# Two-layer attention kernel: the last projection's input turned by VectorE and memory instead of TensorE

## The chip, the cores and the metric

The kernel runs on one core of a Trainium2 chip, in float32. The metric is the device time of one execution in microseconds. The core has five engines with their own instruction streams: TensorE (PE, matmuls; PEld is its weight load), VectorE (DVE), ScalarE (ACT), GpSimd (POOL) and SyncE (SP), which here only issues DMAs.

## The reference

Two layers over the same 8192 tokens of 512 channels. The change concerns the end of the second layer:

```
x = layer0(x)                     # group norm, 8-head attention over 1024 tokens, residual
# layer 1, for each of 8 images (b) of 1024 positions:
x_ln = layernorm(x); q = x_ln @ wq + bq
o = gelu(depthwise 7x7 conv of q, stride 2); offsets = 1x1 conv of o; sample x at 256 points
k, v from the samples; att = softmax(q_h k_h^T) v_h       # 8 heads of 64
z = att @ mo_w + mo_b + x
out = gelu(layernorm(z) @ mlp_w + mlp_b) + z
```

## The kernel before, in words

There are two passes. The first computes layer 0 for all images and leaves its output in memory (mid) and a normalised copy (hat_d). The second pass, where the change is, works on 16 half images (hi) of 512 positions and in each on 4 pairs of heads, so on 64 units. Unit n takes a pair of heads: scores (TensorE), the row maxima (VectorE), exponentials (ScalarE), then `moved`: the 128x1024 exponentials are transposed by VectorE in 32x32 blocks into sq, written to memory (sq_d) and read back (et) so that keys lie on partitions. This happens twice a unit, for the two heads. `share` and `spread` do the same with the sums of the softmax (rsT, rs_d, inv). `product` (av) multiplies et by the values, and `scale` writes attH. The tiles et and sq have two buffers each.

What follows attention for a half image is done four units later, one tile of 128 positions per unit, by `back_steps`: `fetch` and `add` bring the residual (xr), `joined` multiplies attH by wo, adds xr into z and takes mean and variance on VectorE, the power on GpSimd; `norm` makes zn; `turned` transposes zn with four TensorE transposes and two ScalarE copies into zT; `mlp` multiplies zT by wm; `biased`, `gelu` and `end` finish. The last half image is done after the last unit ("tail").

Nothing is scheduled by priority. Each step is put into a list with a place (`at(place, step)`), the list is sorted by place, and each engine and each DMA queue runs its instructions in that order. In unit n the scores stand at n, the transposes and moves of the two heads at n+0.02 and n+0.04, the sums between them, wo at n+0.05, the next queries (wqq) at n+0.06, zn at n+0.13, av of unit n at n+1.1, `turned` at n+0.6, and `mlp` at n+1.03, right behind the scores of unit n+1. Convolution fills, keys and values for the next image stand between av and the scores of some units. In every queue an instruction that waits holds up all behind it; SyncE issues sq_d, et, rs_d, inv, xr and the loads of the next operands.

All instructions pass one helper, line 54, so the profile names them by tile.

Of the kernel before, what the change touches and what calls it, by code (L numbers as in the profile page):

```python
# [9 lines left out]
F32 = mybir.dt.float32  # L10
I32 = mybir.dt.int32
AF = mybir.ActivationFunctionType
ALU = mybir.AluOpType
# [4 lines left out]
P = 128  # L18
# [3 lines left out]
C = 512  # L22
NC = C // P
# [11 lines left out]
SQ = 32  # L35
NSQ = P // SQ
# [30 lines left out]
class Attention:  # L67
# [14 lines left out]
    @staticmethod  # L82
    def by_blocks(keys):

        return keys.rearrange("p (j q s) -> p s j q", s=NSQ, q=SQ)
# [104 lines left out]
class MovedAttention(Attention):  # L190
# [34 lines left out]
    def part(self, et, v, half, first):  # L225
        if half == 0 and first:
            self.av = self.ps_av.tile([P, QB], F32, tag="av", name="av")
        av = self.av[:, ts(half, 2 * P)].rearrange("p (n r q) -> p r n q", n=2, q=SQ)
        for j in range(0 if first else NQT, NQT if first else NT):
            for h in range(2):  # L230
                self.nc.tensor.matmul(
                    av[ds(h * HD, HD)],
                    lhsT=v[not first][:, j % NQT, ds(h * HD, HD)],
                    rhs=et[:, h, :, j],
                    start=(j == 0),
                    stop=(j == NT - 1),
                )
# [3 lines left out]
def attention_then_deformable_attention(  # L241
# [30 lines left out]
    nc = tc.nc  # L272
# [4 lines left out]
    dram = ctx.enter_context(tc.tile_pool(name="dram", bufs=1, space=DRAM))  # L277
# [4 lines left out]
    ident = const.tile([P, P], F32, tag="ident", name="ident")  # L282
# [7 lines left out]
    def mm_tile():  # L290
        return ps_mm.tile([P, QB], F32, tag="mm", name="mm")

    def by_chunk(w):
        return w.rearrange("(c p) o -> p c o", p=P)

    def load_w(pool, w, name):
        t = pool.tile([P, NC, w.shape[1]], F32, tag=name, name=name)
        nc.sync.dma_start(t, by_chunk(w))
        return t
# [43 lines left out]
    def rstd(dst, var, eps):  # L343
        nc.vector.tensor_scalar(dst, var, eps, None, ALU.add)
        nc.gpsimd.tensor_tensor(dst, dst, minus_half[:, 0 : dst.shape[1]], ALU.pow)

    def project(lhsT, rhs):
        ps = mm_tile()
        out = ps[:, 0 : rhs(0).shape[-1]]
        for c in range(NC):  # L350
            nc.tensor.matmul(out, lhsT=lhsT(c), rhs=rhs(c), start=(c == 0), stop=(c == NC - 1))
        return out
# [4 lines left out]
    def at(place, step):  # L357
        due.append((place, len(due), step))
# [37 lines left out]
    with ExitStack() as l0:  # L396
# [3 lines left out]
        nc = InOrder(tc)  # L400
# [25 lines left out]
        def load_weight(w):  # L426
# [17 lines left out]
            out=g3, in_=g3, pattern=[[-GRP, ng], [0, GRP]], compare_op=ALU.is_ge,  # L444
# [3 lines left out]
            out=g3, in_=g3, pattern=[[GRP, ng], [0, GRP]], compare_op=ALU.is_ge,  # L448
# [318 lines left out]
        for b in range(B):  # L767
            first = b * per
            for hp in range(1, NHP):
                places = first_places if b == 0 else pair_places  # L770
# [17 lines left out]
            for hp in range(NHP):  # L788
                for qt in range(NT):
                    n = first + hp * NT + qt  # L790
                    if n % per == 0 and b > 0:
# [6 lines left out]
                    t = qkv[b, hp]  # L798
# [5 lines left out]
                        q=t["q", qt // NQT][:, ts(qt % NQT, P)],  # L804
                        k=t["k"],
# [7 lines left out]
    with ExitStack() as l1:  # L813
        nc = tc.nc


        def pool(name, bufs=1):
            return l1.enter_context(tc.tile_pool(name=name, bufs=bufs, reuse_waits="tile"))

        first, raw, late, late2, cv, cvhat, wp = (  # L820
            pool(n) for n in ("first", "raw", "late", "late2", "cv", "cvhat", "w2")
        )
        work = pool("work1", 2)
        nc = InOrder(tc)
# [4 lines left out]
        bqq, bvk, bvv, bv_c, bq_c, lng, lnb = (  # L829
            wp.tile([P, NC], F32, tag=n, name=n)  # L830
            for n in ("bqq", "bvk", "bvv", "bv_c", "bq_c", "lng", "lnb")
        )
        dwb = cv.tile([P, NC], F32, tag="dwb", name="dwb")
        dww = cv.tile([P, NC, KS * KS], F32, tag="dww", name="dww")
        pww = cv.tile([P, NC, 2], F32, tag="pww", name="pww")

        def load_small():
            with nc.allow_non_contiguous_dma(reason="small vectors onto partitions"):
                for t, v in (
                    (bvk, mk_b), (bv_c, bv), (bvv, mv_b), (bqq, mq_b), (bq_c, bq), (lng, ln_g),  # L840
                    (lnb, ln_b),
                ):
                    nc.sync.dma_start(t, v.rearrange("(c p) -> p c", p=P))

        def load_conv():
            with nc.allow_non_contiguous_dma(reason="small vectors onto partitions"):
# [221 lines left out]
        def tmp(name, bufs):  # L1068
            return work.tile([P, C], F32, tag=name, name=name, bufs=bufs)

        def back_steps(hi, start, step, tail=False):

            b, half = divmod(hi, 2)
            xs = mid[b].rearrange("(t p e) c -> e t p c", e=2, p=P)[half]
            outs = out_tok[b].rearrange("(t p e) c -> e t p c", e=2, p=P)[half]
            xr, z, zn, zT, res = {}, {}, {}, {}, {}
            n_units = 2 * B * NHP

            def fetch(t):
                xr[t] = tmp("xr", 4)  # L1080
                nc.sync.dma_start(xr[t], xs[t])

            def add(t):
                nc.gpsimd.tensor_tensor(xr[t], xr[t], bo_row, ALU.add)

            def joined(t):
                ps = project(lambda c: attH[hi][:, c, ts(t, P)], lambda c: wo[:, c, :])
                z[t] = tmp("z", 4)
                nc.vector.tensor_tensor(z[t], ps, xr[t], ALU.add)
                stats = work.tile([P, 6], F32, tag="stats", name="stats")  # L1090
                mv = xr["mv", t] = work.tile([P, 3], F32, tag="mv", name="mv")
                nc.vector.bn_stats(stats, z[t])
                nc.vector.bn_aggr(mv[:, 0:2], stats)
                rstd(mv[:, 2:3], mv[:, 1:2], 1e-5)

            def norm(t):
                zn[t], mv = tmp("zn", 2), xr["mv", t]
                nc.vector.tensor_scalar(
                    zn[t], z[t], mv[:, 0:1], mv[:, 2:3], ALU.subtract, ALU.mult
                )  # L1100

            def turned(t):
                ps = mm_tile()
                for c in range(NC):
                    nc.tensor.transpose(ps[:, ts(c, P)], zn[t][:, ts(c, P)], ident)
                zT[t] = tmp("zT", 2)
                for half in range(2):
                    nc.scalar.copy(zT[t][:, ts(half, C // 2)], ps[:, ts(half, C // 2)])

            def mlp(t):  # L1110
                res["ps", t] = project(lambda c: zT[t][:, ts(c, P)], lambda c: wm[:, c, :])

            def biased(t):
                res[t] = tmp("res", 3)
                nc.vector.tensor_tensor(res[t], res["ps", t], bm_row, ALU.add)

            def gelu(t):
                nc.scalar.activation(res[t], res[t], AF.Gelu)

            def end(t):  # L1120
                (nc.vector if tail else nc.gpsimd).tensor_tensor(res[t], res[t], z[t], ALU.add)
                (nc.sync if tail else nc.gpsimd).dma_start(outs[t], res[t])

            for t in range(NC):
                over, eve = (start + step * t >= n_units - i and not tail for i in range(2))
                n, pair = start + step * t, start + step * (t - t % 2)

                ends = (n + 0.6, n + 1.03, n + 1.035)
                if eve:
                    ends = (n + 0.61, n + 0.72, n + 0.73) if over else (n + 1.06, n + 1.62, n + 1.625)  # L1130
                places = (pair - 1.6, pair - 0.5), (n + 0.05, n + 0.13), ends
                if tail:
                    turn = n + 0.15 + 0.005 * (t > 0)
                    places = (n - 0.7, n - 0.6), (n, n + 0.01), (turn, n + 0.25, n + 0.26)
                steps = (fetch, add), (joined, norm), (turned, mlp, biased)
                for place, what in zip(sum(places, ()), sum(steps, ())):
                    at(place, lambda t=t, what=what: what(t))


                ends = [t - 1, t] if t % 2 and not tail else [t] if tail else []  # L1140

                for what, after in (
                    (gelu, 0.27 if tail else 0.735 if over else 1.72),
                    (end, 0.28 if tail else 0.74 if over else 2.24),
                ):
                    for i in ends:
                        at(n + after, lambda i=i, what=what: what(i))
# [71 lines left out]
        def load_late():  # L1219
            nonlocal bq_row, wo, wm, bo_row, bm_row  # L1220
            bq_row = load_row(wp, bq, "bq_row")
            wo = load_w(late2, mo_w, "wo")
            wm = load_w(late2, mlp_w, "wm")
            bo_row = load_row(late, mo_b, "bo_row")
            bm_row = load_row(late2, mlp_b, "bm_row")
            load_conv()
# [66 lines left out]
```

## Time and profile before

| | |
|---|---|
| median of 3 runs | 3526.83 us (3524.01 to 3528.84) |
| profiled execution | 3522.86 us, span 3521.2 us, mean granted TensorE clock 0.984 |
| busy, share of the span | PE 96%, DVE 72%, ACT 51%, POOL 44% |
| second pass | about 2200 us to the end; its 64 units from about 2297 us to 3477 us |
| DMA | 641.65 MB in all, mean 182 GB/s |

Times in views are microseconds from the start of the span. A row of the groups gives the operation by tiles (out<-in), the shape, the count, busy time and mean ns of one, and the idle time of the engine before them with what ended it. A row of waits gives the total, the count and the longest. A row of a timeline gives start, length, engine and operation; several equal ones are merged, and in square brackets stands the idle time before it. A float32 matmul shows as two records.

### The profile page before, as it was taken

How to read it: one execution, taken by the hardware profiler on the slowest of the kernel's cores; microseconds unless marked ns; L12 is line 12 of the kernel's file. 1: busy time of each engine (PE TensorE's matmuls, PEld its weight loads, DVE VectorE, ACT ScalarE, POOL GpSimd, SP SyncE). 2: the span in 40 equal slices, each digit the busy share in tenths (PEclk: the TensorE clock that was granted, in tenths of full speed). 3: DMA queues.
4: the chain of work that ended last, by engine and by line, in shares of the span. 5: the costliest groups of instructions: out<-in, count | busy, mean ns of one | idle time of the engine just before them, and what ended most of it. 6: DMA issues, size and time to landing. Idle time of an engine off the chain costs nothing.

```text
span 3521.2 us, 45344 instructions
## 1 busy us (share of the span) xinstructions
PE 3388.6 (96%) x14568; PEld 1679.5 (48%) x14568; DVE 2534.7 (72%) x3373; ACT 1809.8 (51%) x3919; POOL 1536.3 (44%) x1903
## 2 busy tenths in 40 slices
PE   7999999999999999999999998889998989899998
PEld 4544554554554554455455444534444444444443
DVE  4767778888888888788888875257777676665654
ACT  3443355566566566566567562245555455554442
POOL 1001226646636646655654653215445353532222
PEclk9999999999999999999999999899999999999999
DMA  4666667766766666767766667445656555565653
GB/s 145 171 159 176 193 170 195 211 160 184 219 164 186 207 169 185 204 174 194 203 174 175 202 177 208 136 157 194 198 175 196 171 181 178 179 199 189 222 184 123
DMA packets 446589, 641.65 MB, mean 182 GB/s; under 512 B 77104, under 2 KB 240944, under 8 KB 444304
## 3 DMA queue, kind: packets, MB, share of 16 engines
q1 hardware_dynamic: 415712, 536.67, 52.4%
q0 software_dynamic: 29488, 100.00, 9.5%
q8 instruction: 116, 1.90, 0.2%
q10 hardware_dynamic: 1152, 2.10, 0.2%
q14 instruction: 121, 0.99, 0.1%
HBM read 246.38 MB, written 123.73 MB: 105 GB/s over the span
## 4 chain that ended last, share of the span: by engine, by line
PE 81%; POOL 4%; ACT 4%; DVE 4%; issue 3%; DMA 2%; SPq 2%; POOLq 0%; ACTq 0%; DVEq 0%
PE mm L54 51%; PE sc L54 16%; PE av L54 15%; ACT e L54 2%; SPq L54 2%; POOL chunk L54 1%; POOL row L54 1%; DVE chunk L54 1%; ACT L54 1%; DVE nmax L54 1%; POOL oa L54 0%; DMA et<-sq_d 0%; DMA sq_d<-sq 0%; POOL rows L54 0%; POOL hat L54 0%
## 5 line engine op out<-in xcount | busy, mean ns | idle before, releaser
L54 ACT ACTIVATE e<-sc,nmax 128x1024 f32<-128x1024 f32 (+1 forms) x1024 | 802.9, 797 | 597.1 <-DVE nmax L54 595.8
L54 DVE TENSOR_REDUCE nmax<-sc 128x1 f32<-128x1024 f32 (+1 forms) x640 | 751.4, 1215 | 383.7 <-PE sc L54 382.7
L54 DVE STREAM_TRANSPOSE sq<-e 128x1024 f32<-128x1024 f32 x640 | 764.3, 1224 | 241.4 <-ACT e L54 218.2
L54 POOL TENSOR_TENSOR oa<-part_x,oa 128x256 f32<-128x256 f32 x852 | 632.2, 742 | 574.7 <-ACT part_x L54 530.3
L54 PE MATMUL sc<-k,q 64*128 64x512 f32 x2048 | 536.6, 619 | 17.1 <-ACT e L54 15.4
L54 ACT ACTIVATE part_x<-pad_x,dww_x 128x256 f32<-128x256 f32 x852 | 434.9, 541 | 222.9 <-POOL oa L54 221.3
L54 PE MATMUL av<-et,v 128*64 128x256 f32 x4096 | 503.5, 388 | 13.9 <-DMA et<-sq 13.0
L54 PE MATMUL mm<-xT,wqkv 128*128 128x512 f32 x1024 | 470.6, 604 | 3.1 <-issue 3.1
L54 PEld LDWEIGHTS av<-et,v 128*64 128x64 f32 x4096 | 275.3, 137 | 319.2 <-issue 161.2
L54 POOL TENSOR_TENSOR chunk<-parts,chunk 128x256 f32<-128x256 f32 x240 | 179.9, 749 | 384.3 <-ACT parts L54 369.2
L54 PEld LDWEIGHTS sc<-k,q 64*128 64x128 f32 x2048 | 186.5, 187 | 280.0 <-issue 190.7
L54 PEld LDWEIGHTS mm<-xT,wqkv 128*128 128x128 f32 x1024 | 187.1, 190 | 240.3 <-issue 234.9
L54 POOL TENSOR_TENSOR mv<-mv,minus_half 128x1 f32<-128x1 f32 x128 | 77.3, 604 | 489.2 <-DVE mv L54 487.1
L54 PEld LDWEIGHTS mm<-wqkv,xT 128*128 128x128 f32 x2048 | 234.1, 192 | 25.7 <-issue 25.7
L54 PE MATMUL mm<-wqkv,xT 128*128 128x128 f32 x2048 | 244.8, 278 | 0.0
L54 PE MATMUL mm<-wm,zT 128*128 128x512 f32 x512 | 238.1, 608 | 1.3 <-ACT zT L54 1.0
L54 PE MATMUL mm<-w,attT 128*128 128x512 f32 x512 | 235.5, 604 | 1.7 <-DVE attT L54 1.7
L54 PE MATMUL mm<-wo,attH 128*128 128x512 f32 x512 | 230.8, 593 | 0.4
L54 PE MATMUL mm<-hat_h,wqq 128*128 128x512 f32 x512 | 230.7, 593 | 0.0
L54 DVE SCALAR_TENSOR_TENSOR od<-pad_x,dww_x,od 128x256 f32<-128x256 f32 x276 | 226.4, 820 | 5.5
L54 ACT ACTIVATION_READ_ACCUMULATOR e<-sc,nmax 128x1 f32 x1024 | 209.2, 204 | 0.0
L54 PE MATMUL mm<-w,hat_x 128*128 128x512 f32 x384 | 172.7, 600 | 0.0
(163 smaller groups left out, 3555.4 us busy)
## 6 DMA issues: line engine op xcount, KB each, us to landing
et<-sq SPq DMA_DIRECT2D x2048, 128.0 KB
sq_d<-sq SPq DMA_DIRECT2D x128, 512.0 KB
et<-sq_d SPq DMA_DIRECT2D x128, 512.0 KB
inv<-rs_d SPq DMA_DIRECT2D x256, 128.0 KB
hat_h<-hat_d SPq DMA_DIRECT2D x16, 1024.0 KB
xr<-mid SPq DMA_DIRECT2D x64, 256.0 KB
x<-in_x_dram POOLq DMA_DIRECT2D x60, 256.0 KB
out_dram<-res POOLq DMA_DIRECT2D x60, 256.0 KB
```

The source lines that it names most:

```text
L54: return self.tc.keep_in_program_order(op(*args, **kwargs))
```

## The change

For all but the last half image, `turned` transposes zn on VectorE in 32x32 blocks into zT and writes it to memory (z_d); `back` reads it back into zT so that channels lie on partitions, channel s*128 + c*32 + k on partition 4k + s. wm, lng and lnb are loaded in that order of channels, by four DMAs each. zT holds its four chunks interleaved, so the lhsT of `mlp` is read with a stride of four elements. The last half image keeps the TensorE transposes, with zn and the copies written in the new order. `turned` moves from n+0.6 to n+0.1301 and `back` stands at n+0.3; `mlp` stays, but for the last units.

```diff
+        def by_parts(v):
+            return [
+                v[ts(s, NC * SQ)].rearrange("(c k) o -> k c o" if len(v.shape) > 1 else "(c k) -> k c", k=SQ)
+                for s in range(NSQ)
+            ]
...
-                    (bvk, mk_b), (bv_c, bv), (bvv, mv_b), (bqq, mq_b), (bq_c, bq), (lng, ln_g),
-                    (lnb, ln_b),
+                    (bvk, mk_b), (bv_c, bv), (bvv, mv_b), (bqq, mq_b), (bq_c, bq),
                 ):
                     nc.sync.dma_start(t, v.rearrange("(c p) -> p c", p=P))
+                for t, v in ((lng, ln_g), (lnb, ln_b)):
+                    for s, part in enumerate(by_parts(v)):
+                        nc.sync.dma_start(t[ds(s, SQ, NSQ)], part)
...
             def norm(t):
                 zn[t], mv = tmp("zn", 2), xr["mv", t]
+                out, row = zn[t], z[t]
+                if tail:
+                    out, row = by_blocks(out, "(c k s)"), by_blocks(row, "(s c k)")
                 nc.vector.tensor_scalar(
-                    zn[t], z[t], mv[:, 0:1], mv[:, 2:3], ALU.subtract, ALU.mult
+                    out, row, mv[:, 0:1], mv[:, 2:3], ALU.subtract, ALU.mult
                 )
+            def by_blocks(row, order):
+                return row.rearrange(f"p {order} -> p s c k", s=NSQ, c=NC)
             def turned(t):
-                ps = mm_tile()
-                for c in range(NC):
-                    nc.tensor.transpose(ps[:, ts(c, P)], zn[t][:, ts(c, P)], ident)
                 zT[t] = tmp("zT", 2)
-                for half in range(2):
-                    nc.scalar.copy(zT[t][:, ts(half, C // 2)], ps[:, ts(half, C // 2)])
+                if tail:
+                    ps = mm_tile()
+                    for c in range(NC):
+                        nc.tensor.transpose(ps[:, ts(c, P)], zn[t][:, ts(c, P)], ident)
+                    for half in range(2):
+                        nc.scalar.copy(
+                            part(t)[:, ds(2 * half, 2)],
+                            ps[:, ts(half, C // 2)].rearrange("p (c q) -> p c q", q=P),
+                        )
+                    return
+                nc.vector.transpose(
+                    zT[t].rearrange("p (s q c) -> p s c q", s=NSQ, c=NC),
+                    zn[t].rearrange("p (s c k) -> p s c k", s=NSQ, c=NC),
+                )
+                there = zT["there", t] = dram.tile([P, NSQ, P], F32, tag="z_d", name="z_d", bufs=3)
+                nc.sync.dma_start(there, zT[t].rearrange("p (s x) -> p s x", s=NSQ))
+            def back(t):
+                if not tail:
+                    nc.sync.dma_start(
+                        zT[t].rearrange("p (r x) -> p r x", r=NSQ),
+                        zT["there", t].rearrange("(r k) s x -> (k s) r x", r=NSQ),
+                    )
+            def part(t):
+                return zT[t].rearrange("p (q c) -> p c q", c=NC)
             def mlp(t):
-                res["ps", t] = project(lambda c: zT[t][:, ts(c, P)], lambda c: wm[:, c, :])
+                res["ps", t] = project(lambda c: part(t)[:, c], lambda c: wm[:, c, :])
...
-                ends = (n + 0.6, n + 1.03, n + 1.035)
-                if eve:
-                    ends = (n + 0.61, n + 0.72, n + 0.73) if over else (n + 1.06, n + 1.62, n + 1.625)
+                ends = (n + 0.1301, n + 0.3, n + 1.03, n + 1.035)
+                if eve and not over:
+                    ends = (n + 0.1301, n + 0.3, n + 1.62, n + 1.625)
+                elif over:
+                    ends = (n + 0.1301, n + 0.3, n + 0.72, n + 0.73)
...
-                    places = (n - 0.7, n - 0.6), (n, n + 0.01), (turn, n + 0.25, n + 0.26)
-                steps = (fetch, add), (joined, norm), (turned, mlp, biased)
+                    places = (n - 0.7, n - 0.6), (n, n + 0.01), (turn, turn, n + 0.25, n + 0.26)
+                steps = (fetch, add), (joined, norm), (turned, back, mlp, biased)
...
-            wm = load_w(late2, mlp_w, "wm")
+            wm = late2.tile([P, NC, C], F32, tag="wm", name="wm")
+            for s, part in enumerate(by_parts(mlp_w)):
+                nc.sync.dma_start(wm[ds(s, SQ, NSQ)], part)
```

## The prediction

> **What bounds the kernel now.** I read the page's engine totals and chain first, then for the second pass (windows from 2400 to 3400 us) the groups by shape and the waits of the SyncE queue, and last two units instruction by instruction.
>
> ```profile
> PE 3388.6 (96%) x14568; PEld 1679.5 (48%) x14568; DVE 2534.7 (72%) x3373; ACT 1809.8 (51%) x3919; POOL 1536.3 (44%) x1903
> ```
>
> ```profile
> L54 PE MATMUL mm<-ident,zn 128*128 128x128 f32 x212 | 36.0, 296 | 38.2 <-DVE zn L54 38.2
> ```
>
> TensorE is the bound, and the transposes cost it their own work and 38.2 us of waiting for zn in 53 tiles. SyncE's queue is the second thing to read:
>
> ```profile
> SPq L54 <- DMA sq_d<-sq: 420.4, 106, 9.7
> SPq L54 <- DVE sq L54: 261.0, 46, 11.2
> SPq L54 <- PE av L54: 81.3, 33, 5.3
> ```
>
> SyncE waits 106 times, 4 us each, for a write to memory to land before it may issue the read back, and 33 times for the av products: et has two buffers, so the first et read of unit n needs the end of av of unit n-1. One unit in the queue (3374.50 to the next unit's sq_d):
>
> ```profile
> 3374.50 0.38 SPq L54 DMA_DIRECT2D et<-sq_d  x1
> 3374.93 0.50 SPq L54 DMA_DIRECT2D rs_d<-rsT  x1
> 3375.47 0.42 SPq L54 DMA_DIRECT2D sq_d<-sq  x1
> 3379.99 0.37 SPq L54 DMA_DIRECT2D et<-sq_d  x1
> 3380.40 1.24 SPq L54 DMA_DIRECT2D inv<-rs_d  x2
> 3381.74 1.02 SPq L54 DMA_DIRECT2D xr<-mid  x2
> ```
>
> and the same stretch on TensorE:
>
> ```profile
> 3373.45 1.03 PE L54 MATMUL av<-et,vals 128*64 128x512 f32 x4
> 3374.40 2.08 PE L54 MATMUL mm<-smp,wvk 128*128 128x256 f32 x8
> 3376.32 0.60 PE L54 MATMUL mm<-ident,zn 128*128 128x128 f32 x4
> 3376.85 2.00 PE L54 MATMUL sc<-keys,q 64*128 64x256 f32 x16
> 3378.78 3.70 PE L54 MATMUL mm<-wm,zT 128*128 128x512 f32 x8
> 3382.32 3.60 PE L54 MATMUL mm<-wo,attH 128*128 128x512 f32 x8
> 3385.75 3.60 PE L54 MATMUL mm<-hat_h,wqq 128*128 128x512 f32 x8
> 3389.28 1.94 PE L54 MATMUL av<-et,vals 128*64 128x512 f32 x8
> ```
>
> The et read leaves 0.02 us after av ends (3374.48). The mlp product follows the scores directly, 4.30 us after av's end here. From mlp's start to av's end is 12.44 us of TensorE without a gap.
>
> **What the change removes.** 60 of 64 tiles lose four transposes. From transpose to scores is 0.53 us (3376.32 to 3376.85): 60 x 0.53 = 32 us, and the 38 us of waits. ACT loses 120 copies of 377 ns, off the path.
>
> **What it adds on VectorE.** 60 block transposes of 128x512. sq<-e does 128x1024 in 1224 ns, so 0.61 us; the output here has a stride of four elements, which no row shows, so up to twice that. It follows zn directly, before attH and the convolution taps. VectorE is busy 715 of 1065 us from 2385 to 3450 us, so it has the room, and SyncE comes to the tile later than this (below): nothing taken.
>
> **What it adds on SyncE: a loop.** The issue order puts z_d<-zT and zT<-z_d of unit n behind sq_d, et, rs_d, sq_d, et, inv, inv of unit n. The first et waits for av of unit n-1. TensorE's own order is scores n+1, mlp n, wo, wqq, av n, and mlp n needs zT. So each mlp waits for a chain that starts at the end of the previous av, and each av waits for that mlp. What lies between av and scores (transposes before; keys, values, fills still) can hide in the wait, but the loop itself cannot be shorter than its terms:
>
> - TensorE from mlp to the end of av: 12.44 us.
> - av's end to et: 0.02; et to the end of the second inv issue: 3381.64 - 3374.50 = 7.14, of which 4.52 is the second sq_d landing.
> - z_d, next in the queue: 0.10 later. Write of 256 KB to its landing: the completion events of mid<-xr, 256 KB in the first pass, give 2.85 us; sq_d, 512 KB, gives 4.5. It queues behind an et and two inv still in flight, so 3.7.
> - Queue to the read, 0.10. zT read, 256 KB in 512-byte runs: the inv pairs move as much in such runs in 3.4 to 3.7 us each in the first pass; xr, 256 KB, takes 5.4 behind other reads. The queue ahead is empty then, so 4.0. To TensorE 0.05.
> - The clock. TensorE now idles some 10 us in each loop. What that costs stands in two places of before:
>
> ```profile
> 2558.78 1.12 PE L54 MATMUL mm<-ident,zn 128*128 128x128 f32 x4 [4.33 <-DVE zn L54]
> 2559.82 3.79 PE L54 MATMUL sc<-keys,q 64*128 64x256 f32 x16
> 2563.54 3.80 PE L54 MATMUL mm<-wm,zT 128*128 128x512 f32 x8
> ```
>
> After an idle of 4.33 us the transposes took 1.12 instead of 0.60 and the scores 3.79 instead of 2.00; the granted clock from 2559 to 2562 us is 0.50. That is 2.3 us lost; shorter cases in the trace lost 1.2. I take 2.3 in each loop.
>
> Sum: 12.44 + 0.02 + 7.14 + 0.10 + 3.7 + 0.10 + 4.0 + 0.05 + 2.3 = 29.85 us. Before, 57 loops lie from the mlp of unit 5 (2389.75) to that of unit 62 (3453.18): 1063.4 / 57 = 18.66. So 57 x 11.19 = 638 us more.
>
> The Trainium skill, "DMA: Bandwidth & Descriptors", section "Anatomy of one DMA — SWDGE (gpsimd) path", gives a DMA 2.0 us plus its bytes at 436 GB/s, so, as an estimate, 2.6 us for each of the two. The completion events here say 2.85 and 3.4 at the least; by the page the loop would be 2.5 us shorter and the kernel 143 us faster than my sum.
> The same skill, "TensorE: Matmul & The Clock Gate", section "What's actually happening", reopens the clock after one busy window of about 3.4 us, which would lose 1.7 us in a loop instead of the 2.3 that the rows show: 34 us less.
>
> **Edges.** The first mlp (unit 5) waits until 2391.98 (end of its inv) + 7.9 instead of 2389.75: +10. At the end the last two tiles come 15 and 19 us after the last loop's av, about where the et waits put them before: +2. In the tail four zn write, and eight copies write, with strides: 0 to 1 us a tile, +2. Before the loop, 9 more DMA issues at about 0.5 us stand ahead of later weights: 0 to 4.5, +1. zT is read as lhsT with a stride of four: the weight load of 190 ns hides under a matmul pitch of 430; smp as weights at stride 2 takes 196, so nothing, and up to 1.5 us a unit if it doubled. Together +15.
>
> 3522.86 (profiled execution) + 638 + 15 = 4176; the median of the runs lies 4 us above the profiled one: 4180.
>
> **Rivals.** (1) Faster: the round trip is hidden and TensorE only gets shorter: 3527 - 32 - 38 = 3457. It decides if zT lands within 2 us of av's end (plus what lies between av and scores, 0 to 7 us). For it: 96% TensorE. Against: z_d is not even issued until 7.2 us after av's end. 4%. (2) The latency is exposed but not the queue, as if z_d left at once: wo's end is 6.97 us after mlp's start, zn ends up to 5 us later, then transpose 0.7 and 7.9 for both DMAs: a loop of 20.5, 57 x 1.8 + 15 = +118, 3645. Against it the issue order on SyncE. 6%. (3) The clock stays low for the whole section of TensorE: 12.44 us becomes 24.9, the loop 40, 4750. Against: in the case shown the wo product after 8 us is back at 3.60. 3%. No change (within 0.2%) needs gain and wait to cancel: 1%. My case: 86%.
>
> **Range.** With 2.85, 3.4 and 1.2 us for write, read and clock the loop is 27.3: 4037. With 4.5, 5.4 and a full low stretch of 6.8 us (3.4 lost) it is 33.2: 4375; all three high at once is unlikely, so 4320. Runs agree within 0.2%, which is what can be told from no change.
>
> **What would show it.** Right: the mlp matmuls wait for DMA zT<-z_d in nearly every unit, 8 to 13 us; the et read still 0.02 us after av; z_d 7.2 us after that; unit period 27 to 33 us and nearly constant; granted clock down to some 0.7 in this stage; zn waits gone. Wrong: z_d issued before et, mlp waiting under 3 us, or TensorE still above 90% there.

## The result, and the profile after

The changed kernel takes 4185.43 us (median of 4 runs, 4183.69 to 4190.22) against 3526.45 us: ratio 1.187, 95% interval 1.185 to 1.189. Its profiled execution has a span of 4182.5 us, 661 us more than before, and a mean granted TensorE clock (the share of its full clock that the profile says TensorE was given) of 0.912 instead of 0.984.

The page of after: engine totals, the clock by 40 slices (in tenths), and the chain that ended last, which is followed back from the last instruction, at each step to what released it:

```profile
PE 3468.5 (83%) x14328; PEld 1706.5 (41%) x14328; DVE 2596.6 (62%) x3433; ACT 1775.9 (42%) x3799; POOL 1534.2 (37%) x1903
PEclk9999999999999999999999887887878887787888
PE 72%; DMA 17%; DVE 4%; SPq 3%; issue 2%; POOL 2%; ACT 1%; POOLq 0%; DVEq 0%; ACTq 0%
```

The same line of before:

```profile
PE 81%; POOL 4%; ACT 4%; DVE 4%; issue 3%; DMA 2%; SPq 2%; POOLq 0%; ACTq 0%; DVEq 0%
```

The first pass is as before; from the 23rd slice on the clock is between 0.7 and 0.9 (0.81 on the mean from 2400 to 4060 us), and DMAs, 2% of the chain before, are 17% of it. The waits of TensorE, then of SyncE's queue, from 2400 to 4060 us (total us, times, longest):

```profile
PE mm L54 <- DMA zT<-z_d: 591.1, 56, 16.7
```

```profile
SPq L54 <- PE av L54: 589.5, 55, 14.4
SPq L54 <- DMA sq_d<-sq: 513.4, 111, 10.5
SPq L54 <- DMA z_d<-zT: 220.8, 56, 6.6
```

Two waits of the same length face each other: TensorE waits 591 us for SyncE's read, and SyncE waits 590 us for TensorE's av. That is a loop. One turn of it, on TensorE (the dots stand for lines left out) and on SyncE:

```profile
3302.00 5.29 PE L54 MATMUL mm<-wm,zT 128*128 128x512 f32 x8 [12.79 <-DMA zT<-z_d]
3307.12 3.60 PE L54 MATMUL mm<-wo,attH 128*128 128x512 f32 x8
3310.55 3.60 PE L54 MATMUL mm<-hat_h,wqq 128*128 128x512 f32 x8
3314.08 1.94 PE L54 MATMUL av<-et,vals 128*64 128x512 f32 x8
...
3331.90 5.69 PE L54 MATMUL mm<-wm,zT 128*128 128x512 f32 x8 [11.40 <-DMA zT<-z_d]
```

```profile
3316.04 0.37 SPq L54 DMA_DIRECT2D et<-sq_d  x1
3316.51 0.45 SPq L54 DMA_DIRECT2D rs_d<-rsT  x1
3317.05 0.38 SPq L54 DMA_DIRECT2D sq_d<-sq  x1
3322.30 0.37 SPq L54 DMA_DIRECT2D et<-sq_d  x1
3322.76 1.24 SPq L54 DMA_DIRECT2D inv<-rs_d  x2
3324.09 0.55 SPq L54 DMA_DIRECT2D z_d<-zT  x1
3328.21 0.38 SPq L54 DMA_DIRECT2D zT<-z_d  x1
```

av ends at 3316.02; et leaves 0.02 us later; z_d leaves only at 3324.09, its landing (the completion event of the DMA) releases zT at 3328.21, and mlp starts at 3331.90, 29.90 us after the mlp before it. From the mlp of unit 5 (2404.12) to that of unit 62 (4112.50) lie 57 turns of 29.97 us on the mean.

### The profile page after: what moved, and what is told of

It is laid out like the page before. It is cut to its first block, busy times and chain, and to the rows that moved or that the text cites. A ratio compares the mean times of both kernels' runs of the same rounds, so it can differ in the third digit from the quotient of the medians.

```text
span 4182.5 us, 45127 instructions
## 1 busy us (share of the span) xinstructions
PE 3468.5 (83%) x14328; PEld 1706.5 (41%) x14328; DVE 2596.6 (62%) x3433; ACT 1775.9 (42%) x3799; POOL 1534.2 (37%) x1903
## 4 chain that ended last, share of the span: by engine, by line
PE 72%; DMA 17%; DVE 4%; SPq 3%; issue 2%; POOL 2%; ACT 1%; POOLq 0%; DVEq 0%; ACTq 0%
PE mm L54 47%; PE av L54 13%; PE sc L54 12%; DMA z_d<-zT 6%; DMA sq_d<-sq 5%; DMA zT<-z_d 4%; SPq L54 3%; DVE smp L54 1%; ACT e L54 1%; DVE chunk L54 1%; DVE nmax L54 1%; DVE attH L54 1%; DMA et<-sq 1%; POOL oa L54 0%; POOL rows L54 0%
## 5 line engine op out<-in xcount | busy, mean ns | idle before, releaser
L54 PE MATMUL mm<-wm,zT 128*128 128x512 f32 x512 | 369.3, 886 | 618.3 <-DMA zT<-z_d 616.8
L54 PEld LDWEIGHTS mm<-wm,zT 128*128 128x128 f32 x512 | 160.3, 324 | 805.0 <-issue 765.4
L54 DVE TENSOR_TENSOR res<-mm,bm_row 128x512 f32<-128x512 f32 x64 | 44.2, 691 | 560.1 <-PE mm L54 560.0
L54 ACT ACTIVATE q<-mm,bqq 128x512 f32<-128x512 f32 x64 | 44.0, 688 | 813.8 <-PE mm L54 813.8
```

What stands on the lines that cost most here:

```text
L54: return self.tc.keep_in_program_order(op(*args, **kwargs))
```

## The experiments

The theory (the expectations call it the queue theory): the unit is 30 us long because zT's trip stands in SyncE's queue behind an et read that waits for the previous av. The rivals: the latency of two DMAs in a row wherever they stand; the added traffic; the layout (strided weights and transposes). "Before" is the kernel before in runs on the same chip.

### The trip ahead of the heads' DMAs (e2_order)

`moved` keeps the VectorE transpose; a new step `sent` holds its sq_d write and et read.

```diff
             at(n + 0.02, lambda: att.moved(u, 0))
             at(n + 0.039, lambda: att.share(u["sums"]))
             at(n + 0.04, lambda: att.moved(u, 1))
-            at(n + 0.041, lambda: u.update(inv=att.spread()))
+            at(n + 0.31, lambda: att.sent(u, 0))
+            at(n + 0.32, lambda: att.sent(u, 1))
+            at(n + 0.33, lambda: u.update(inv=att.spread()))
```

> Only SyncE's order is changed: in each unit the writes and reads of the two heads (sq_d, et) and the inv reads are issued behind z_d and zT instead of ahead of them. Queue theory: what makes the unit 30 us is that zT's trip stands behind an et read that waits for the previous av. With it in front, z_d leaves when zT is transposed: mlp to the end of wo 7.0 us, z to the end of the transpose about 4.8, write 4.2, read 3.1, a little for the clock: 19 to 20.5 us a unit, total 3560 to 3660 us. Rival, the latency itself (two DMAs in a row cost what they cost wherever they stand): unchanged, about 4185. Rival, traffic (31 MB more in short runs): unchanged, about 4185.

Measured: 3657.46 us, ratio 1.038 (1.036 to 1.040), inside the range at its upper end. From the scores of unit 5 to those of unit 63 a unit takes 20.38 us. TensorE's waits from 2400 to 3400 us, and SyncE's queue in one unit:

```profile
PE mm L54 <- DMA zT<-z_d: 80.7, 29, 6.8
```

```profile
2932.95 0.32 SPq L54 DMA_DIRECT2D z_d<-zT  x1
2938.29 0.37 SPq L54 DMA_DIRECT2D zT<-z_d  x1
2938.70 0.51 SPq L54 DMA_DIRECT2D sq_d<-sq  x1
2942.28 0.37 SPq L54 DMA_DIRECT2D et<-sq_d  x1
```

The same DMAs with the same bytes cost 528 us less when zT does not stand behind et. Both rivals said that this order would change nothing, and fall as causes of the 660 us. Part of the gain is that the write itself lands sooner here: from z_d's issue to zT's are 2.90 us on the mean instead of 4.50 in the changed kernel. The 134 us over before that are left are what the trip costs in this place, its two DMAs in a row, the clock that the waits let fall and the heads' DMAs that now stand behind it, less what the change saves; this run does not split them.

### The mlp one unit later (e3_later)

```diff
-                ends = (n + 0.1301, n + 0.3, n + 1.03, n + 1.035)
+                ends = (n + 0.1301, n + 0.3, n + 2.03, n + 2.035)
...
-                zT[t] = tmp("zT", 2)
+                zT[t] = tmp("zT", 3)
...
-                zn[t], mv = tmp("zn", 2), xr["mv", t]
+                zn[t] = work.tile([P, C], F32, tag="q", name="zn") if tail else tmp("zn", 1)
+                mv = xr["mv", t]
...
-                    (gelu, 0.27 if tail else 0.735 if over else 1.72),
-                    (end, 0.28 if tail else 0.74 if over else 2.24),
+                    (gelu, 0.27 if tail else 0.735 if over else 2.4),
+                    (end, 0.28 if tail else 0.74 if over else 2.6),
```

> The mlp step of a tile, and what follows it, stands one unit later (behind the scores of unit n+2), with one zT buffer more and one zn buffer less. The DMAs and their order are those of the change. Queue theory: zT lands 15.2 us after av's end and TensorE gets to the mlp 16.3 us or more after it, so the wait on zT goes from 591 us to under 60. SyncE's queue in itself needs about 17 us a unit (four waits for a landing in a row), so the unit is 17.3 to 18.7 us: 3440 to 3540 us in all. Rival, traffic: the same bytes move, so at least half of the loss stays: above 3800 us.

Measured: 3560.03 us, ratio 1.010 (1.007 to 1.013), 20 us over the expected range; a unit takes 19.07 us. TensorE's waits from 2400 to 3400 us:

```profile
PE av L54 <- DMA et<-sq_d: 37.9, 16, 4.3
PE mm L54 <- DMA zT<-z_d: 5.8, 7, 1.9
```

The wait on zT is gone, as the theory has it, and 210 GB/s move in that stretch, against 135 GB/s in the changed kernel and 186 before: traffic was not the limit. What is left is the queue itself: from 2400 to 3400 us SyncE waits 706 us for landings of sq_d and z_d, and for av not at all.

```profile
2900.86 0.37 SPq L54 DMA_DIRECT2D et<-sq_d  x1
2901.33 0.45 SPq L54 DMA_DIRECT2D rs_d<-rsT  x1
2901.88 0.39 SPq L54 DMA_DIRECT2D sq_d<-sq  x1
2906.28 0.37 SPq L54 DMA_DIRECT2D et<-sq_d  x1
2906.70 1.24 SPq L54 DMA_DIRECT2D inv<-rs_d  x2
2908.04 0.55 SPq L54 DMA_DIRECT2D z_d<-zT  x1
2911.93 0.38 SPq L54 DMA_DIRECT2D zT<-z_d  x1
2912.41 0.93 SPq L54 DMA_DIRECT2D xr<-mid  x2
2913.38 0.43 SPq L54 DMA_DIRECT2D sq_d<-sq  x1
2918.44 0.37 SPq L54 DMA_DIRECT2D et<-sq_d  x1
```

From et to et are 17.58 us, and in them SyncE waits for three landings in a row (4.40, 3.89 and 5.06 us from an issue to the next) and for no engine; the next turn has 19.95. The expectation had four such waits in a turn, where there are three, and put the queue at 17 us; the turns are longer than that by 0.6 to 3 us here and by 2 on the mean.

### Without the trip (e4_notrip), and with the transposes on TensorE (e5_pe)

The first leaves out z_d and zT (`turned` ends after the VectorE transpose, `back` does nothing); the second sends every tile the way of the last half image:

```diff
-                if tail:
+                if True:
                     ps = mm_tile()
...
-                ends = (n + 0.1301, n + 0.3, n + 1.03, n + 1.035)
+                ends = (n + 0.6, n + 0.6, n + 1.03, n + 1.035)
```

> The transposes on VectorE stay, the write z_d and the read zT are left out, so the last projection reads blocks that are not on their channels' partitions (that part of the computation is left out). Both theories: what is left of the change is then only its gain: 32 us of transposes and 38 us of waits on TensorE less, 3450 to 3480 us. Rival, the layout (weights read with a stride of four, VectorE's strided transposes of 1.15 us): most of the 660 us would stay.

> All tiles take the way of the last half image: transposes on TensorE, zn and the copies written with a stride, weights in the new order and read with a stride of four; no trip through memory. Queue theory: all this lies beside TensorE's work, 3525 to 3545 us (up to 0.5 us a unit where zn is waited for). Rival, the layout: 4000 us or more.

Measured: e4_notrip 3499.47 us, ratio 0.993 (0.991 to 0.996), 20 us above its range; e5_pe 3534.54 us, ratio 1.003 (1.002 to 1.004), inside. So the strided weights, zn and copies cost 12 us, the transposes on VectorE leave a kernel that is faster than before, and the trip is the whole loss: 4185 - 3499 = 686 us. Why the rest gains 23 us and not the 43 to 73 of the range is in part to be seen in TensorE's waits from 2400 to 3400 us, in before and in e4_notrip:

```profile
PE mm L54 <- DVE zn L54: 38.2, 15, 4.9
PE sc L54 <- ACT q L54: 32.4, 8, 6.8
```

Before had no wait on q there. The transposes' own 32 us are saved, but a wait of nearly the same length stands at the next instruction, the scores, which need the queries' copy from ScalarE. The strided weights add 0.12 us a unit (from mlp to wo 3.66 us instead of 3.54): 7 us.

### The clock by itself (e6_warm)

The list WARM, left out here, has the number of added matmuls for each unit.

```diff
             def mlp(t):
+                if not tail and start + t - 5 < len(WARM):
+                    warm = mm_tile()
+                    for i in range(WARM[start + t - 5]):
+                        nc.tensor.matmul(warm, lhsT=wo[:, i % NC, 0:P], rhs=wo[:, i % NC, :], start=True, stop=True)
                 res["ps", t] = project(lambda c: part(t)[:, c], lambda c: wm[:, c, :])
```

> The change, with 606 matmuls added whose results are dropped: they stand between the scores and the mlp and fill most of each wait (3 to 18 per unit, by the length of the wait in the changed kernel less 1.2 us, at 0.86 us each). If the low clock after the wait costs what the loop's sum says, mlp to the end of av falls from 14.7 to 12.5 us and the unit by 2.2: 57 x 2.2 = 127 us less, 4040 to 4090 us. Rival: the slow mlp is the strided weight load (308 ns instead of 190) and not the clock: 4185 or more.

Measured: 4077.58 us, ratio 1.157 (1.155 to 1.159), inside the range; clock 0.985. A turn with the added matmuls (its lines are numbered one higher):

```profile
3013.11 2.00 PE L55 MATMUL sc<-keys,q 64*128 64x256 f32 x16
3015.04 9.71 PE L55 MATMUL mm<-wo 128*128 128x512 f32 x22
3026.86 3.79 PE L55 MATMUL mm<-wm,zT 128*128 128x512 f32 x8 [2.11 <-DMA zT<-z_d]
3030.49 3.60 PE L55 MATMUL mm<-wo,attH 128*128 128x512 f32 x8
```

mlp takes 3.79 instead of 5.1 to 6.4 us, mlp to the end of av 12.81 on the mean instead of 14.71, and the turn 28.11 instead of 29.97. TensorE does more work and the kernel is 108 us faster. The strided weight load is the same in both, so the slow mlp was the clock.

### z_d earlier (e8_early)

The second head's et read is split off `moved` into a step `read`, which comes behind z_d.

```diff
-            at(n + 0.041, lambda: u.update(inv=att.spread()))
+            at(n + 0.14, lambda: att.read(u, 1))
+            at(n + 0.141, lambda: u.update(inv=att.spread()))
```

> Only SyncE's order: z_d is issued right behind the second sq_d write, ahead of the second et read and the inv reads, so the two writes land together; zT's read stays behind inv. The loop's sum: av's end to zT's issue 7.6 to 8.5 us instead of 12.1, then 3.1 and TensorE's 14.7: 25.5 to 26.5 us a unit, 3920 to 3990 us. Rival, traffic or latency: unchanged, 4185.

Measured: 4084.32 us, ratio 1.160 (1.158 to 1.162), 94 us over the range: 101 us are won of the 195 to 265 expected. SyncE's queue:

```profile
3235.72 0.38 SPq L54 DMA_DIRECT2D z_d<-zT  x1
3239.79 0.37 SPq L54 DMA_DIRECT2D et<-sq_d  x1
3240.29 1.24 SPq L54 DMA_DIRECT2D inv<-rs_d  x2
3241.57 0.60 SPq L54 DMA_DIRECT2D zT<-z_d  x1
```

zT now leaves 7.3 us after the first et, as planned (12.2 in the turn of the changed kernel shown above), but lands in 5.97 us on the mean instead of 2.99. It is issued while an et and two inv reads are still in flight; in the changed kernel the wait for z_d lets those land first, and at 59 of its 60 zT reads no other DMA of SyncE's is in flight. The turn is 28.29 us: 1.7 won of 3.5 to 4.5.

### Both (e7_both)

The edits of e3_later and of e8_early together.

> The mlp one unit later, as in the run of that edit alone, and z_d issued right behind the second sq_d write as in the other: zT then lands about 11 us after av's end, TensorE comes to it 16.3 us after, and SyncE's queue needs only some 13 us a unit. Queue theory: TensorE is the bound again with 14.4 us a unit and what stands between av and scores: 17.2 to 17.6 us, 3440 to 3475 us, faster than both kernels. Rival: VectorE with 1.15 us more a unit, or et landing late behind z_d, becomes the bound: 3527 or more.

Measured: 3500.14 us, ratio 0.993 (0.992 to 0.994): faster than both kernels by 25 us and more, but 25 us above the range. A unit takes 18.03 us. TensorE's waits from 2400 to 3400 us:

```profile
PE sc L54 <- ACT q L54: 22.1, 9, 5.5
PE av L54 <- DMA et<-sq_d: 7.4, 6, 3.7
PE mm L54 <- DMA zT<-z_d: 1.5, 2, 1.1
```

The trip costs nothing that can be seen any more: against before this is 25 us, where e4_notrip without the trip gained 23. The rival falls. The longest wait that is left is that on q, as in e4_notrip.

### The taps behind the queries' copy (e9_q_first, e10_notrip_q)

```diff
-                            place = 0.25 + 0.01 * j if not lane else 0.045 + 0.001 * j if j < 4 else 0.65 + 0.01 * j
+                            place = 0.25 + 0.01 * j if not lane else 0.065 + 0.001 * j if j < 4 else 0.65 + 0.01 * j
```

> The version with the mlp one unit later and z_d issued early, and in each unit the four ScalarE taps of the convolution that stood ahead of the next queries' copy (q) moved behind it. In the version without this the scores waited 22 us for q between 2400 and 3400 us, because ScalarE's queue stood at a tap that waits for GpSimd. If that wait is what is left of the expected gain, it falls by half or more: 3475 to 3495 us. Rival: the taps' delay comes back as later exponentials, or the wait is ScalarE's own length: 3500 or more.

> The version without the trip through memory (its last projection reads unmoved blocks), with the same four taps moved behind q. There the scores waited 32 us for q in the same window, and the time was 3499 instead of 3450 to 3480. If q is the reason, 3460 to 3485 us. Rival: 3495 or more, and what is missing lies elsewhere.

Measured: 3539.19 us, ratio 1.003 (1.002 to 1.004), and 3539.86 us, 1.003 (1.002 to 1.004): both some 35 us slower than without the edit, each taken against before on its own chip (11 and 12 us over it instead of 25 and 23 under it). Both miss their ranges. The waits of TensorE in e9_q_first, same window:

```profile
PE mm L54 <- DVE res L54: 21.6, 5, 6.4
PE mm L54 <- ACT th L54: 18.7, 6, 4.6
PE av L54 <- DMA et<-sq_d: 16.9, 6, 6.2
PE sc L54 <- ACT q L54: 6.5, 3, 2.3
```

and the longest with that on q in e10_notrip_q:

```profile
PE mm L54 <- DVE zT L54: 25.7, 9, 3.7
PE sc L54 <- ACT q L54: 12.1, 7, 3.2
```

The wait on q fell to a third (from 22.1 and 32.4 us), and others rose by more together: in e9_q_first res, th and et by 45 us, in e10_notrip_q zT by 22. The rival holds: the taps' delay comes back elsewhere. So it is not shown that the wait on q is what is missing from the gain of e4_notrip and e7_both; that cause stays open.

## Why the prediction was right

It forecast 4180 us (4037 to 4320); 4185 was measured, and the mechanism is the one it named: TensorE waits for zT 56 times from 2400 to 4060 us, 10.6 us each on the mean (4 to 17, where 8 to 13 were forecast), et still leaves 0.02 us after av, z_d 7.6 us later, every turn takes 28 to 33 us, the clock is at 0.81 (some 0.7 was forecast), and no wait on zn is left. Its terms, beside their means over the 57 turns (from the issues and completion events of the trace):

| term of the turn, us | predicted | measured |
|---|---|---|
| mlp to the end of av, with the clock | 12.44 + 2.3 | 14.71 |
| av's end to et | 0.02 | 0.02 |
| et to the end of the second inv issue | 7.14 | 7.51 |
| to z_d's issue | 0.10 | 0.10 |
| z_d: issue to landing | 3.7 | 4.48 |
| to zT's issue | 0.10 | 0.02 |
| zT: issue to landing, and to mlp | 4.0 + 0.05 | 2.99 + 0.14 |
| turn | 29.85 | 29.97 |

- **The loop** was read off the issue order and one wait of before (33 times, 81 us on av). e2_order shows that this order, not the DMAs themselves, is the cause of 528 of the 659 us.
- **The two DMAs** were off by 0.8 and 1.0 us, with opposite signs. The write is issued with an et and two inv reads in flight, as forecast, and the later of those inv reads lands 3.8 us after its issue on the mean, later than the 3.7 put down for the write; the read had the queue to itself, as forecast, but its 4.0 was taken from reads that ran beside others. The sum hit by luck there; the range did not need it. The low end took 2.85 us for the write, which is near the median of the mid<-xr landings (2.87) and not the least of them (2.48). The estimate of 2.6 us for each from the Trainium skill's fit in "DMA: Bandwidth & Descriptors", "Anatomy of one DMA — SWDGE (gpsimd) path", which is for DMAs that GpSimd issues, is below both means: zT lands in 2.55 us at the least, z_d in 3.81, and e8_early reads zT in 5.97, so the measurement decides.
- **The clock** costs 14.71 - 12.81 = 1.90 us a turn by e6_warm, whose turns still have waits of up to 2.8 us; I had 2.3 from one case of before. In the rows of before the transposes and scores behind a wait of 3.5 to 4.9 us for zn lost between 1.4 and 2.3 us. The estimate of 1.7 us from the Trainium skill, "TensorE: Matmul & The Clock Gate", "What's actually happening", is somewhat nearer to e6_warm.
- **VectorE** takes 1.15 us for a strided transpose, the upper end of what I gave (0.61 to twice that); it stayed covered: e4_notrip, which has it, is faster than before. **The edges** come to 661 - 57 x 11.31 = 16 us, predicted 15. **The strided weights**, put at nothing, cost 0.12 us a unit.
- **Rival 2** (latency without the queue: 20.5 us a unit, 3645 us) is e2_order: 20.38 and 3657. **Rival 1** (hidden: 3457) is nearest to e4_notrip and e7_both, and too good by 43 us: the saving of 38 us of waits on zn was counted as if nothing came late behind it, and waits on q of 32 and 22 us stand in its place. Whether q alone is behind it is not shown.

## What to carry to other kernels

Before a step is moved to a DMA queue, write down what stands ahead of it there, and look for an instruction that waits on the engine which in turn waits for the new step: then the period cannot be shorter than the sum around that loop, though no engine is busy all the time (TensorE 65% here), and the sum can be added up from the rows of the kernel before. In this kernel the round trip through memory fitted in when its consumer was moved a whole unit later and the write was issued before the next wait of its queue (e7_both). A wait taken from one instruction may be found again at the next one of the same engine.

## What the runs showed of the hardware

The weight load of mlp, with its rows read at a stride of four float32 elements, takes 307 ns at the least (before, read densely, 186, and 190 at the median), and its transposes on VectorE, written at that stride, 1.15 us for 512 elements a partition, where sq<-e, written in runs of 32 elements, takes 1.22 for 1024:

```profile
L54 PEld LDWEIGHTS mm<-wm,zT x512: 307/333/338, 2404.1 to 4176.1; 128*128 128x128 f32 x171
L54 DVE STREAM_TRANSPOSE zT<-zn x60: 1077/1151/1201, 2386.9 to 4130.8; 128x512 f32<-128x512 f32 x60
L54 ACT COPY zT<-mm x8: 607/648/692, 4152.9 to 4173.0; 128x256 f32<-128x256 f32 x8
```

Columns are minimum, median and maximum ns. ScalarE's strided copies take 648 ns instead of 378. Little of the three showed in the time: 12 us in e5_pe, which has the weights and the copies, 7 of them by the weight load, which I had expected to be hidden without a row to show it.

The landing time of a DMA depended on what was still in flight on the same queue. The 256 KB read of zT took 2.9 to 3.0 us on the mean in the changed kernel, e2_order and e3_later, where almost always nothing else of SyncE's was in flight at its issue, and 6.0 and 6.2 us in e8_early and e7_both, issued with an et and two inv reads in flight. The 256 KB write of z_d took 4.5 us with those in flight in the changed kernel, and 2.3 us in the 19 units of e2_order that had nothing in flight. By size alone the landings did not go: in the changed kernel, from 2400 to 4060 us, the medians were 3.9 us for 16 KB (rs_d), 4.4 for 128 KB (inv) and 4.2 for 512 KB (et).
